# Causal linear attention: scores issued over four row groups, values kept stationary in four column groups, one PSUM ring of eight

## The chip, the cores and the metric

The kernel runs on one core of a Trainium2 chip. The metric is the device time of one execution in microseconds (us), lower is better. The core has a tensor engine (PE; its weight loads are listed apart as PEld), a vector engine (DVE), a scalar engine (ACT), a general engine (POOL), an engine that only issues transfers here (SP), and DMA engines that move data between device memory and the on-chip memory. Matrix products land in PSUM, from where DVE and ACT read them.

## The reference

The input x has 4 sequences of 1024 tokens with 256 channels. It is normalised, and two parts are added to it: an attention part and a mixture of experts. All arithmetic is in fp32.

```
xn = layernorm(x)
q, k, v = xn @ w_q.T, xn @ w_k.T, xn @ w_v.T        # 16 heads of 16 channels
sq, sk  = elu(q) + 1, elu(k) + 1
# causal linear attention, in chunks of 128 tokens, per head
scores = (sq_chunk @ sk_chunk.T) * lower_triangle
num = scores @ v_chunk + sq_chunk @ S
den = scores.sum(-1) + sq_chunk @ z
local = num / max(den, 1e-6)
S, z = S + sk_chunk.T @ v_chunk, z + sk_chunk.sum(0)
# memory output: sq against a coarse and four fine memories per head, mixed by gates
attn = (gate * memory + (1 - gate) * local) @ w_o.T
# experts: top 2 of 8 (176 hidden channels each), and a shared one with 352
out = x + attn + experts(xn) + shared(xn)
```

## The kernel before

The 4096 tokens are 32 tiles of 128, taken as 8 blocks of 4 tiles; two blocks are one sequence. The 16 heads are split into two halves c of 8 heads, each half on 128 channels (partitions). Head h of a half stands on partitions 16h to 16h+15, so two heads share each of four groups g of 32 partitions.

First all blocks are normalised and routed. Then the tokens are sorted by expert: 64 indirect DMAs on POOL (`scatter`, line 407) write rows to a sorted copy in device memory. There are 71 expert steps (`expert`, lines 779 to 809), each on 128 sorted rows with its own weights, loaded from SP two steps ahead (`fetch`). Each step is a transpose pair (pxg), a product (phe), an activation on ACT and DVE, another transpose pair (pTe) and a product (pye), with ACT copying between them, and its rows go out to device memory. At the end 64 indirect gathers on POOL (`combine`, line 815) bring two expert rows for each token back; DVE adds them and SP stores the result.

Attention of a block (`attention_units`) has four units for each of its tiles i:

- `scores(i)`: for each g, four products, two halves c and two heads r. They contract 16 partitions for the even head; for the odd head they contract 32, with a copy of the keys (skO) that is zero on the even head's rows. One PSUM tile sc holds the four results of a g, 128 keys by 128 queries each. DVE multiplies it with the causal mask into sT (line 535).
- `local(i)`: for each half, the state term, with the queries as the stationary operand and the state streamed (line 550), and then for each head a product with the masked scores as stationary operand (128 by 128) and the head's values and a column of ones, 17 columns, streamed (line 555). All land in one PSUM tile pn with tokens on partitions. DVE clips and inverts the denominators, and scales (lines 564 to 567).
- `update(i)`: keys are transposed, multiplied with the values, masked to each head's own rows on DVE (line 594) and added to the old state on POOL (line 598), except for the first tile of a sequence, which needs no addition.
- `memory(i)`: the products px and py with the memories, scaled on DVE (line 625, tile fm) and added on POOL (lines 630 and 631). fm has one buffer.

After four tiles come `expand_gate` and `mix`, which make the attention result. `shared_units` adds the shared expert and the output projection.

Blocks are overlapped by `together` (line 827): while block b has its shared units and block b+1 its attention, the expert steps of sixths of the 71 are dealt in between (blocks 0 to 5); in blocks 6 and 7 the combines are dealt in. The framework's scheduler then orders the instructions of each engine at compile time and gives each tile a buffer; SP alone keeps the order of the program. Each engine executes its queue in order.

PSUM has two pools of four tiles: ps_a for routing and attention, and ps_f for the experts and the shared part (lines 88 and 89).

Of the kernel before, what the change touches and what calls it, by code (L numbers as in the profile page):

```python
# [8 lines left out]
FP = mybir.dt.float32  # L9
# [5 lines left out]
P = 128  # L15
NT = 4
TB = P * NT
# [5 lines left out]
def linear_attention_moe_kernel(  # L23
# [28 lines left out]
    nc = tc.nc  # L52
    T, H = x.shape
    S = T // B
    NH = memory_gate.shape[1]
    HD = H // NH
    NC = H // P
    HC = NH // NC
    NG = HC // 2
    NM = memories.shape[1]  # L60
    D1 = HD + 1
    FR = E * F
    FT = w_gate.shape[1]
    FS = FT - FR
# [20 lines left out]
    exw = ctx.enter_context(tc.tile_pool(name="exw", bufs=3))  # L85
    exp = ctx.enter_context(tc.tile_pool(name="exp", bufs=2))
    dram = ctx.enter_context(tc.tile_pool(name="dram", bufs=1, space=bass.MemoryType.DRAM))
    ps_a = ctx.enter_context(tc.tile_pool(name="ps_a", bufs=4, space=bass.MemoryType.PSUM))
    ps_f = ctx.enter_context(tc.tile_pool(name="ps_f", bufs=4, space=bass.MemoryType.PSUM))

    st = {}

# [43 lines left out]
    if full < NF:  # L136
# [26 lines left out]
    nc.vector.tensor_reduce(  # L163
        odd, own.rearrange("p (g r) -> p g r", r=2)[:, :, 1], AX.X, ALU.add
    )

    own_s = const.tile([P, NC, HC * D1], FP, tag="own_s", name="own_s")
    for c in range(NC):
# [340 lines left out]
    def attention_units(blk):  # L509
# [6 lines left out]
                st[name, blk] = one.tile([P, NT, H], FP, tag=name, name=f"{name}_{blk}")  # L516

        def scores(i):
            sqT, skT, skO = st["sqT", blk], st["skT", blk], st["skO", blk]
            tok = slice(i * P, (i + 1) * P)  # L520
            for g in range(NG):
                even = slice(32 * g, 32 * g + HD)
                both = slice(32 * g, 32 * g + 2 * HD)
                sc = ps_a.tile([P, NC, 2, P], FP, tag="a", name=f"sc_{blk}_{i}_{g}")
                for c in range(NC):
                    nc.tensor.matmul(  # L526
                        sc[:, c, 0, :], skT[even, c, tok], sqT[even, c, tok],
                        start=True, stop=True,
                    )
                    nc.tensor.matmul(  # L530
                        sc[:, c, 1, :], skO[both, c, tok], sqT[both, c, tok],
                        start=True, stop=True,
                    )
                sT = tmp.tile([P, NC * 2, P], FP, tag="sT", name=f"sT_{blk}_{i}_{g}", bufs=4)
                nc.vector.tensor_mul(  # L535
                    sT,
                    sc.rearrange("p c r t -> p (c r) t"),
                    causal[:, None, :].to_broadcast([P, NC * 2, P]),
                )
                st["sT", g] = sT  # L540

        def local(i):
            sqT, va = st["sqT", blk], st["va", blk]
            tok = slice(i * P, (i + 1) * P)
            started = half > 0 or i > 0
            pn = ps_a.tile([P, 512], FP, tag="a", name=f"pn_{blk}_{i}")
            for c in range(NC):
                at = c * HC * D1
                if started:
                    nc.tensor.matmul(  # L550
                        pn[:, at : at + HC * D1], sqT[:, c, tok], st["state"][:, c, :],
                        start=True, stop=False,
                    )
                for h in range(HC):
                    nc.tensor.matmul(  # L555
                        pn[:, at + h * D1 : at + (h + 1) * D1],
                        st["sT", h // 2][:, c * 2 + h % 2, :],
                        va[:, i, c * HC + h, :],
                        start=not started,
                        stop=(not started) or h == HC - 1,  # L560
                    )
            pn3 = pn[:, : NH * D1].rearrange("p (h k) -> p h k", k=D1)
            rden = small.tile([P, NH], FP, tag="rden", name=f"rden_{blk}_{i}")
            nc.vector.tensor_scalar(rden, pn3[:, :, HD], EPS, None, ALU.max)  # L564
            nc.vector.reciprocal(rden, rden)
            nc.vector.tensor_mul(rden, rden, ungate)
            nc.vector.tensor_mul(
                st["local", blk][:, i, :].rearrange("p (h k) -> p h k", k=HD),
                pn3[:, :, :HD],
                rden[:, :, None].to_broadcast([P, NH, HD]),  # L570
            )

        def update(i):

            if half == BPB - 1 and i == NT - 1:
                return
            skT, va = st["skT", blk], st["va", blk]
            tok = slice(i * P, (i + 1) * P)
            pk = ps_a.tile([P, NC, P], FP, tag="a", name=f"pk_{blk}_{i}")
            for c in range(NC):  # L580
                nc.tensor.transpose(pk[:, c, :], skT[:, c, tok], ident)
            sk = tmp.tile([P, NC, P], FP, tag="sk", name=f"sk_{blk}_{i}")
            nc.scalar.copy(sk, pk)
            pu = ps_a.tile([P, 512], FP, tag="a", name=f"pu_{blk}_{i}")
            for c in range(NC):
                nc.tensor.matmul(  # L586
                    pu[:, c * HC * D1 : (c + 1) * HC * D1],
                    sk[:, c, :],
                    va[:, i, c * HC : (c + 1) * HC, :].rearrange("p h k -> p (h k)"),
                    start=True, stop=True,  # L590
                )
            old = st.get("state") if half > 0 or i > 0 else None
            new = tmp.tile([P, NC, HC * D1], FP, tag="state", name=f"state_{blk}_{i}")
            nc.vector.tensor_mul(  # L594
                new, pu[:, : NC * HC * D1].rearrange("p (c k) -> p c k", c=NC), own_s
            )
            if old is not None:
                nc.gpsimd.tensor_add(new, new, old)  # L598
            st["state"] = new

        def memory(i):
            sqT, w5 = st["sqT", blk], st["w5", b]
# [98 lines left out]
    def shared_units(blk):  # L701
        hid = {}

        def hidden(f):
            xnT = st["xnT", blk]
            n = min(P, FS - f * P)
            pg = ps_f.tile([P, TB], FP, tag="f", name=f"pg_{blk}_{f}")
            pu = ps_f.tile([P, TB], FP, tag="f", name=f"pu_{blk}_{f}")
            for ps, w in ((pg, wg), (pu, wu)):
                for k in range(NC):  # L710
                    nc.tensor.matmul(  # L711
                        ps[:n, :], w[:, k, f * P : f * P + n], xnT[:, k, :],
                        start=(k == 0), stop=(k == NC - 1),
                    )

            th = tmp.tile([P, TB], FP, tag="wide", name=f"th_{blk}_{f}", bufs=3)
            nc.scalar.activation(th[:n], pg[:n], AF.Tanh, scale=0.5)
            nc.vector.scalar_tensor_tensor(  # L718
                th[:n], th[:n], 1.0, pg[:n], ALU.add, ALU.mult
            )  # L720
            h = hidp.tile([P, TB], FP, tag="h", name=f"h_{blk}_{f}")
            nc.vector.scalar_tensor_tensor(  # L722
                h[:n], th[:n], 0.5, pu[:n], ALU.mult, ALU.mult
            )
            hid[f] = h

        def output(i):
            tok = slice(i * P, (i + 1) * P)
            rows = slice(blk * TB + i * P, blk * TB + (i + 1) * P)
            oT = st["oT", blk]  # L730
            if i == 0:
                st["acc", blk] = big.tile([P, NT, H], FP, tag="tok", name=f"acc_{blk}")
            res = tmp.tile([P, H], FP, tag="res", name=f"res_{blk}_{i}")
            nc.scalar.dma_start(res, x[rows, :])
            po = ps_f.tile([P, 512], FP, tag="f", name=f"po_{blk}_{i}")
            for c in range(NC):
                nc.tensor.matmul(  # L737
                    po[:, :H], oT[:, c, tok], wo[:, c, :], start=(c == 0), stop=False
                )
            for f in range(NF):  # L740
                n = min(P, FS - f * P)
                nc.tensor.matmul(  # L742
                    po[:, :H], hid[f][:n, tok], wd[:n, f, :],
                    start=False, stop=(f == NF - 1),
                )
            nc.vector.tensor_add(st["acc", blk][:, i, :], po[:, :H], res)
# [32 lines left out]
    def expert(j):  # L779
        rows = slice(j * P, (j + 1) * P)  # L780
        fetch(j + 2)
        wgu, wdn, xg = st.pop(("fetched", j))
        pt = ps_f.tile([P, NC, P], FP, tag="f", name=f"pxg_{j}")
        for c in range(NC):
            nc.tensor.transpose(pt[:, c, :], xg[:, c * P : (c + 1) * P], ident)
        xgT = exp.tile([P, NC, P], FP, tag="xgT", name=f"xgT_{j}")
        nc.scalar.copy(xgT, pt)  # L787
        ph = ps_f.tile([P, 2, F], FP, tag="f", name=f"phe_{j}")
        for k in range(NC):
            nc.tensor.matmul(  # L790
                ph.rearrange("p g f -> p (g f)"), xgT[:, k, :],
# [4 lines left out]
        nc.scalar.activation(th, ph[:, 0, :], AF.Tanh, scale=0.5)  # L796
        nc.vector.scalar_tensor_tensor(th, th, 1.0, ph[:, 0, :], ALU.add, ALU.mult)  # L797
        nc.vector.scalar_tensor_tensor(th, th, 0.5, ph[:, 1, :], ALU.mult, ALU.mult)
        pT = ps_f.tile([P, 2, P], FP, tag="f", name=f"pTe_{j}")
        for f in range(2):  # L800
            nc.tensor.transpose(pT[:FH, f, :], th[:, f * FH : (f + 1) * FH], ident)
        hT = exp.tile([FH, 2, P], FP, tag="hTe", name=f"hTe_{j}")
        nc.scalar.copy(hT, pT[:FH])  # L803
        py = ps_f.tile([P, H], FP, tag="f", name=f"pye_{j}")
        for f in range(2):
            nc.tensor.matmul(py, hT[:, f, :], wdn[:, f, :], start=(f == 0), stop=(f == 1))  # L806
        y = exp.tile([P, H], FP, tag="row", name=f"y_{j}", bufs=5)
# [119 lines left out]
```

## Time and profile before

| what | value |
|---|---|
| median of 14 runs | 1132.08 us (1130.59 to 1143.23) |
| the profiled execution | 1128.23 us, span 1126.5 us |
| PE busy | 1010.0 us, 90% |
| DVE, POOL and ACT busy | 468.2, 237.4 and 210.1 us |
| mean granted clock of PE | 0.831 |
| value products, line 555 | 1024 records, mean 327 ns, busy 186.4 us |
| score products, lines 526 and 530 | 1024 records, busy 87.7 and 83.4 us |
| state term, line 550 | 112 records, busy 35.2 us |
| causal mask, line 535 | 128 instructions, mean 685 ns |

The span runs from the first to the last instruction of the program. "Granted clock" is the share of full speed at which PE was allowed to run. Busy time of a group is the union of its instructions' intervals; since matmuls are pipelined, groups that follow each other closely overlap, and their busy times add up to more than the time that passed. What a step takes on PE is better read from when its records start. The chain of waits is followed back from the last instruction: each piece is what the next one waited for.

### The profile page before, as it was taken

To read this page: it belongs to the slowest core of one execution; us is meant where nothing else is said; L and a number is where in the kernel's file an instruction comes from. 1 tells how busy PE (TensorE), PEld (TensorE's weight loads), DVE (VectorE), ACT (ScalarE), POOL (GpSimd) and SP (SyncE) were. 2 spreads that over 40 slices of the span, in tenths; PEclk is the share of its full clock that TensorE was granted. 3 is DMA by queue.
4 is the path that set the end of the run, shared out by engine and by line. 5 is a ranking of instruction groups with operands and counts; after the bars stand their busy time and mean duration, and the time that the engine had idled before them with its cause. 6 is when DMAs were issued, how large, how long until landed. Compare 5 with 4: busy or idle time off the path is not lost.

```text
span 1126.5 us, 13616 instructions
## 1 busy us (share of the span) xinstructions
PE 1010.0 (90%) x4644; PEld 754.3 (67%) x4644; DVE 468.2 (42%) x1382; ACT 210.1 (19%) x522; POOL 237.4 (21%) x261
## 2 busy tenths in 40 slices
PE   4879419899799999999899999899989999999986
PEld 3757317688466787677656788578746788667653
DVE  5775114342333434434343334432333424435765
ACT  1222000101234112111134210221124311110010
POOL 1117772010100011001100011100110001106865
PEclk9998657576899768997899876997699866898888
DMA  9713230112224212232223321232132421102345
GB/s 294 254 54 107 103 115 24 36 45 58 86 68 126 83 37 64 57 93 73 84 67 112 100 73 42 62 101 74 58 86 82 122 74 42 49 24 82 119 135 146
DMA packets 105234, 98.86 MB, mean 88 GB/s; under 512 B 10781, under 2 KB 101069, under 8 KB 105165
## 3 DMA queue, kind: packets, MB, share of 16 engines
q1 hardware_dynamic: 81181, 65.41, 20.0%
q0 software_dynamic: 6144, 16.79, 4.8%
q10 hardware_dynamic: 17840, 15.79, 4.4%
q8 instruction: 37, 0.61, 0.2%
q14 instruction: 32, 0.26, 0.1%
HBM read 66.75 MB, written 31.20 MB: 87 GB/s over the span
## 4 chain that ended last, share of the span: by engine, by line
PE 76%; POOL 9%; DVE 7%; issue 3%; DMA 3%; ACT 2%; ACTq 0%; POOLq 0%; DVEq 0%
PE pn L555 14%; PE phe L790 10%; POOL xs L407 5%; PE pye L806 5%; PE sc L526 5%; PE py L624 4%; PE po L742 3%; PE sc L530 3%; PE pu L711 3%; PE pl L293 2%; PE pg L711 2%; PE pn L550 2%; PE po L737 2%; PE px L606 2%; PE pu L586 2%
## 5 line engine op out<-in xcount | busy, mean ns | idle before, releaser
L555 PEld LDWEIGHTS pn<-va,sT 128*128 128x128 f32 x1024 | 192.4, 283 | 4.1 <-issue 1.5
L555 PE MATMUL pn<-va,sT 128*128 128x17 f32 x1024 | 186.4, 327 | 0.0
L790 PE MATMUL phe<-wgu,xgT 128*128 128x352 f32 x284 | 125.7, 574 | 2.7 <-ACT xgT L787 2.4
L526 PE MATMUL sc<-sqT,skT 16*128 16x128 f32 x512 | 87.7, 309 | 40.3 <-DVE fm L625 39.6
L630 POOL TENSOR_TENSOR fm<-fm 128x512 f32<-128x512 f32 x32 | 40.6, 1269 | 347.3 <-DVE fm L625 188.2
L535 DVE TENSOR_TENSOR sT<-sc,causal 128x512 f32<-128x512 f32 x128 | 84.7, 685 | 62.5 <-PE sc L530 62.0
L526 PEld LDWEIGHTS sc<-sqT,skT 16*128 16x128 f32 x512 | 64.2, 192 | 61.4 <-DVE fm L625 41.9
L790 PEld LDWEIGHTS phe<-wgu,xgT 128*128 128x128 f32 x284 | 61.1, 234 | 38.3 <-issue 14.0
L530 PE MATMUL sc<-sqT,skO 32*128 32x128 f32 x512 | 83.4, 282 | 0.0
L806 PE MATMUL pye<-wdn,hTe 88*128 88x256 f32 x284 | 81.0, 410 | 1.0 <-ACT hTe L803 0.9
L564 DVE TENSOR_SCALAR rden<-pn 128x16 f32<-128x16 f32 x32 | 5.6, 174 | 176.7 <-PE pn L555 176.7
L598 POOL TENSOR_TENSOR state<-state,state 128x272 f32<-128x272 f32 x24 | 18.5, 770 | 280.7 <-DVE state L594 212.5
L624 PE MATMUL py<-mem_y,sqT 128*128 128x512 f32 x128 | 72.3, 669 | 0.0
L407 POOL DMA_INDIRECT xs<-x,is x64 | 61.8, 965 | 41.6 <-DVE is L392 22.4
L530 PEld LDWEIGHTS sc<-sqT,skO 32*128 32x128 f32 x512 | 66.4, 195 | 6.1 <-issue 6.1
L806 PEld LDWEIGHTS pye<-wdn,hTe 88*128 88x128 f32 x284 | 54.1, 201 | 24.0 <-ACT hTe L803 15.4
L815 POOL DMA_INDIRECT yt<-ys,is x64 | 62.2, 971 | 22.4 <-DVE acc L821 8.6
L797 DVE SCALAR_TENSOR_TENSOR the<-the,phe 128x176 f32<-128x176 f32 x71 | 23.7, 334 | 100.1 <-ACT the L796 100.0
L625 DVE TENSOR_TENSOR fm<-py,rw 128x512 f32<-128x512 f32 x64 | 43.6, 682 | 42.6 <-POOL fine L631 40.1
L796 ACT ACTIVATE the<-phe 128x176 f32<-128x176 f32 x71 | 22.6, 318 | 184.7 <-PE phe L790 181.2
L711 PE MATMUL pg<-xnT,wg 128*128 128x512 f32 (+1 forms) x96 | 51.5, 661 | 5.4 <-DVE th L718 5.4
L742 PE MATMUL po<-wd,h 128*128 128x256 f32 (+1 forms) x192 | 48.3, 386 | 2.0 <-DVE h L722 2.0
(174 smaller groups left out, 1446.3 us busy)
## 6 DMA issues: line engine op xcount, KB each, us to landing
wgu<-in_w_gate_dram SPq DMA_DIRECT2D x71, 176.0 KB
wgu<-in_w_up_dram SPq DMA_DIRECT2D x71, 176.0 KB
wdn<-in_w_down_dram SPq DMA_DIRECT2D x71, 176.0 KB
xs<-zero SPq DMA_DIRECT2D x71, 128.0 KB
xg<-xs SPq DMA_DIRECT2D x71, 128.0 KB
ys<-y ACTq DMA_DIRECT2D x71, 128.0 KB
x<-in_x_dram SPq DMA_DIRECT2D x8, 512.0 KB
res<-in_x_dram ACTq DMA_DIRECT2D x32, 128.0 KB
```

The source lines that it names most:

```text
L407: put = nc.gpsimd.indirect_dma_start(out=xs, out_offset=bass.IndirectOffsetOnAxis(ap=islot[r][:, i : i + 1], axis=0), in_=st["x", i // NT] ...
L526: nc.tensor.matmul(sc[:, c, 0, :], skT[even, c, tok], sqT[even, c, tok], start=True, stop=True,)
L530: nc.tensor.matmul(sc[:, c, 1, :], skO[both, c, tok], sqT[both, c, tok], start=True, stop=True,)
L535: nc.vector.tensor_mul(sT, sc.rearrange("p c r t -> p (c r) t"), causal[:, None, :].to_broadcast([P, NC * 2, P]),)
L555: nc.tensor.matmul(pn[:, at + h * D1 : at + (h + 1) * D1], st["sT", h // 2][:, c * 2 + h % 2, :], va[:, i, c * HC + h, :], start=not start ...
L624: nc.tensor.matmul(py, sqT[:, c, tok], mem_y[:, c, :], start=True, stop=True)
L625: nc.vector.tensor_mul(fm[:, c].rearrange("p m (h k) -> p (m h) k", k=HD), py.rearrange("p (n k) -> p n k", k=HD), rw[:, c, HC:, None].to_ ...
L711: nc.tensor.matmul(ps[:n, :], w[:, k, f * P : f * P + n], xnT[:, k, :], start=(k == 0), stop=(k == NC - 1),)
L742: nc.tensor.matmul(po[:, :H], hid[f][:n, tok], wd[:n, f, :], start=False, stop=(f == NF - 1),)
L790: nc.tensor.matmul(ph.rearrange("p g f -> p (g f)"), xgT[:, k, :], wgu[:, k].rearrange("p g f -> p (g f)"), start=(k == 0), stop=(k == NC ...
L806: nc.tensor.matmul(py, hT[:, f, :], wdn[:, f, :], start=(f == 0), stop=(f == 1))
L815: nc.gpsimd.indirect_dma_start(out=yt, out_offset=None, in_=ys, in_offset=bass.IndirectOffsetOnAxis(ap=islot[r][:, i : i + 1], axis=0),)
```

## The change

The change edits the scores, the local step and the state, and joins the PSUM pools.

- `scores(i)` takes four PSUM tiles at once, one for each g, and goes through halves c and heads r outside and g inside, so that four successive products lie in four different groups of 32 partitions. The masks follow after all sixteen products.
- `local(i)` swaps the operands. The heads are taken in four quarters q of four heads. For each quarter the state is stationary (128 by 128: four heads of 32 columns, 17 of them used) and the queries are streamed. For each head the values (128 by 17) are stationary and the masked scores, 128 columns, are streamed; the four heads of a quarter write to partitions 0, 32, 64 and 96 of pn. pn now has channels on partitions, so ACT copies it out, and four transposes bring it back into a new PSUM tile pb, from where DVE goes on as before.
- The state lives in two fixed buffers with 32 columns a head, cleared by POOL at the start. The first tile of a sequence uses the zeros; at the end of a sequence the next buffer is cleared again by POOL. `update` writes every other buffer and always adds the old one.
- One PSUM pool of eight tiles serves everything.

```diff
+    CW = 32
...
-    ps_a = ctx.enter_context(tc.tile_pool(name="ps_a", bufs=4, space=bass.MemoryType.PSUM))
-    ps_f = ctx.enter_context(tc.tile_pool(name="ps_f", bufs=4, space=bass.MemoryType.PSUM))
+    ps_a = ctx.enter_context(tc.tile_pool(name="ps_a", bufs=8, space=bass.MemoryType.PSUM))
+    ps_f = ps_a
...
+    states = [
+        const.tile([P, NC, HC, CW], FP, tag=f"state{k}", name=f"state{k}") for k in range(2)
+    ]
+    for state in states:
+        nc.gpsimd.memset(state, 0.0)
...
+            sc = [
+                ps_a.tile([P, NC, 2, P], FP, tag="a", name=f"sc_{blk}_{i}_{g}")
+                for g in range(NG)
+            ]
+            for c in range(NC):
+                for r, keys in enumerate((skT, skO)):
+                    for g in range(NG):
+                        rows = slice(32 * g, 32 * g + (1 + r) * HD)
+                        nc.tensor.matmul(
+                            sc[g][:, c, r, :], keys[rows, c, tok], sqT[rows, c, tok],
+                            start=True, stop=True,
+                        )
...
+            state = states[(half * NT + i) % 2]
+            nq = NH // 4
+            pn = ps_a.tile([P, nq, P], FP, tag="a", name=f"pn_{blk}_{i}")
+            for q in range(nq):
+                c, h0 = divmod(4 * q, HC)
+                nc.tensor.matmul(
+                    pn[:, q, :],
+                    state[:, c, h0 : h0 + 4, :].rearrange("p h k -> p (h k)"),
+                    sqT[:, c, tok],
+                    start=(q == 0), stop=False, skip_group_check=True,
+                )
+            for q in range(nq):
+                for r in range(4):
+                    c, h = divmod(4 * q + r, HC)
...
+                        pn[CW * r : CW * r + D1, q, :],
+                        va[:, i, c * HC + h, :],
+                        st["sT", h // 2][:, c * 2 + h % 2, :],
+                        start=False, stop=(q == nq - 1), skip_group_check=True,
...
+            nT = tmp.tile([P, nq, P], FP, tag="wide", name=f"nT_{blk}_{i}", bufs=3)
+            nc.scalar.copy(nT, pn)
+            pb = ps_a.tile([P, nq, P], FP, tag="a", name=f"pb_{blk}_{i}")
+            for q in range(nq):
+                nc.tensor.transpose(pb[:, q, :], nT[:, q, :], ident)
+            pn3 = pb.rearrange("p q (r k) -> p (q r) k", k=CW)
...
+            if n == BPB * NT - 1:
+                nc.gpsimd.memset(new, 0.0)
                 return
...
+            nc.gpsimd.tensor_add(
+                new[:, :, :, :D1], new[:, :, :, :D1], old[:, :, :, :D1]
+            )
```

More of the change, by code (lines that the diff above doesn't have):

```diff
@@ L520, in scores @@
             tok = slice(i * P, (i + 1) * P)
-            for g in range(NG):
[L522 to L533, printed above, removed]
+            sc = [
[10 more added lines that the diff above has]
+                        )
+            for g in range(NG):
                 sT = tmp.tile([P, NC * 2, P], FP, tag="sT", name=f"sT_{blk}_{i}_{g}", bufs=4)
@@ L536, in scores @@
                     sT,
-                    sc.rearrange("p c r t -> p (c r) t"),
+                    sc[g].rearrange("p c r t -> p (c r) t"),
                     causal[:, None, :].to_broadcast([P, NC * 2, P]),
@@ L544, in local @@
             tok = slice(i * P, (i + 1) * P)
[L545 to L549, printed above, removed]
+            state = states[(half * NT + i) % 2]
[12 more added lines that the diff above has]
+                    c, h = divmod(4 * q + r, HC)
                     nc.tensor.matmul(
-                        pn[:, at : at + HC * D1], sqT[:, c, tok], st["state"][:, c, :],
-                        start=True, stop=False,
-                    )
[L554 to L562, printed above, removed]
+                        pn[CW * r : CW * r + D1, q, :],
+                        va[:, i, c * HC + h, :],
+                        st["sT", h // 2][:, c * 2 + h % 2, :],
+                        start=False, stop=(q == nq - 1), skip_group_check=True,
+                    )
+            nT = tmp.tile([P, nq, P], FP, tag="wide", name=f"nT_{blk}_{i}", bufs=3)
[4 more added lines that the diff above has]
+            pn3 = pb.rearrange("p q (r k) -> p (q r) k", k=CW)
             rden = small.tile([P, NH], FP, tag="rden", name=f"rden_{blk}_{i}")
@@ L573, in update @@
         def update(i):
-            if half == BPB - 1 and i == NT - 1:
+            n = half * NT + i
+            old, new = states[n % 2], states[(n + 1) % 2]
+            if n == BPB * NT - 1:
+                nc.gpsimd.memset(new, 0.0)
                 return
@@ L591, in update @@
                 )
-            old = st.get("state") if half > 0 or i > 0 else None
-            new = tmp.tile([P, NC, HC * D1], FP, tag="state", name=f"state_{blk}_{i}")
             nc.vector.tensor_mul(
-                new, pu[:, : NC * HC * D1].rearrange("p (c k) -> p c k", c=NC), own_s
-            )
-            if old is not None:
-                nc.gpsimd.tensor_add(new, new, old)
-            st["state"] = new
+                new[:, :, :, :D1],
+                pu[:, : NC * HC * D1].rearrange("p (c h k) -> p c h k", c=NC, k=D1),
+                own_s.rearrange("p c (h k) -> p c h k", k=D1),
+            )
+            nc.gpsimd.tensor_add(
+                new[:, :, :, :D1], new[:, :, :, :D1], old[:, :, :, :D1]
+            )
         def memory(i):
@@ L706, in hidden @@
             n = min(P, FS - f * P)
-            pg = ps_f.tile([P, TB], FP, tag="f", name=f"pg_{blk}_{f}")
-            pu = ps_f.tile([P, TB], FP, tag="f", name=f"pu_{blk}_{f}")
+            pg = ps_f.tile([P, TB], FP, tag="a", name=f"pg_{blk}_{f}")
+            pu = ps_f.tile([P, TB], FP, tag="a", name=f"pu_{blk}_{f}")
             for ps, w in ((pg, wg), (pu, wu)):
@@ L734, in output @@
             nc.scalar.dma_start(res, x[rows, :])
-            po = ps_f.tile([P, 512], FP, tag="f", name=f"po_{blk}_{i}")
+            po = ps_f.tile([P, 512], FP, tag="a", name=f"po_{blk}_{i}")
             for c in range(NC):
@@ L782, in expert @@
         wgu, wdn, xg = st.pop(("fetched", j))
-        pt = ps_f.tile([P, NC, P], FP, tag="f", name=f"pxg_{j}")
+        pt = ps_f.tile([P, NC, P], FP, tag="a", name=f"pxg_{j}")
         for c in range(NC):
@@ L787, in expert @@
         nc.scalar.copy(xgT, pt)
-        ph = ps_f.tile([P, 2, F], FP, tag="f", name=f"phe_{j}")
+        ph = ps_f.tile([P, 2, F], FP, tag="a", name=f"phe_{j}")
         for k in range(NC):
@@ L798, in expert @@
         nc.vector.scalar_tensor_tensor(th, th, 0.5, ph[:, 1, :], ALU.mult, ALU.mult)
-        pT = ps_f.tile([P, 2, P], FP, tag="f", name=f"pTe_{j}")
+        pT = ps_f.tile([P, 2, P], FP, tag="a", name=f"pTe_{j}")
         for f in range(2):
@@ L803, in expert @@
         nc.scalar.copy(hT, pT[:FH])
-        py = ps_f.tile([P, H], FP, tag="f", name=f"pye_{j}")
+        py = ps_f.tile([P, H], FP, tag="a", name=f"pye_{j}")
         for f in range(2):
```

## The prediction

> **What bounds the kernel now.** I read the page's busy times first, then the chain of waits, then windows, and last the timeline of single steps.
>
> ```profile
> PE 1010.0 (90%) x4644; PEld 754.3 (67%) x4644; DVE 468.2 (42%) x1382; ACT 210.1 (19%) x522; POOL 237.4 (21%) x261
> PEclk9998657576899768997899876997699866898888
> PE 76%; POOL 9%; DVE 7%; issue 3%; DMA 3%; ACT 2%; ACTq 0%; POOLq 0%; DVEq 0%
> PE pn L555 14%; PE phe L790 10%; POOL xs L407 5%; PE pye L806 5%; PE sc L526 5%; PE py L624 4%; PE po L742 3%; PE sc L530 3%; PE pu L711 3%; PE pl L293 2%; PE pg L711 2%; PE pn L550 2%; PE po L737 2%; PE px L606 2%; PE pu L586 2%
> ```
>
> The tensor engine carries three quarters of the chain. The value products (pn, line 555) are its largest item, and the scores (sc, lines 526 and 530) and the state term (line 550) are edited too. The granted clock is often near half.
>
> ```profile
> 165.00:1020.00 855.00, 820.10 (x3794) 613.91 (x3794) 320.03 (x838) 175.60 (x446) 87.30 (x88) 0.83 0.25 70
> 543.80:547.20 3.40, 3.40 (x18) 3.40 (x18) 0.00 (x0) 0.00 (x0) 0.00 (x0) 0.50 0.00 0
> 343.00:363.00 20.00, 20.00 (x79) 12.78 (x77) 6.42 (x17) 10.68 (x27) 0.00 (x0) 1.00 0.45 125
> ```
>
> These are windows: length, then busy time of PE, weight loads, DVE, ACT and POOL, granted clock, DMA. From 165 to 1020 us PE idles only 35 us of 855. Inside a value step (second line) the clock is 0.50; in a stretch of projections and experts it is 1.00. Mean 0.83 means 2 x 0.17 x 855 = 291 us at half clock.
>
> ```profile
> 517.82 3.44 PE L555 MATMUL pn<-va,sT 128*128 128x17 f32 x16
> 479.05 1.86 PE L555 MATMUL pn<-va,sT 128*128 128x17 f32 x16
> ```
>
> Each fp32 matmul leaves two records (1024 for 512 in the page's groups), a transpose one. Sixteen records take 3.23 us on the chain at half clock (202 ns each); the full-clock example takes 1.86 us, about 110 each. Only 17 columns stream: the 128-column weight load sets this pace.
>
> ```profile
> 535.90 0.37 PE L530 MATMUL sc<-sqT,skO 32*128 32x128 f32 x1
> 535.90 0.37 PE L526 MATMUL sc<-sqT,skT 16*128 16x128 f32 x1
> 536.11 0.27 PE L530 MATMUL sc<-sqT,skO 32*128 32x128 f32 x1
> 536.12 0.27 PE L526 MATMUL sc<-sqT,skT 16*128 16x128 f32 x1
> 536.23 0.38 PE L530 MATMUL sc<-sqT,skO 32*128 32x128 f32 x2
> 536.45 0.49 PE L526 MATMUL sc<-sqT,skT 16*128 16x128 f32 x4
> 536.67 0.49 PE L530 MATMUL sc<-sqT,skO 32*128 32x128 f32 x4
> 537.01 0.38 PE L526 MATMUL sc<-sqT,skT 16*128 16x128 f32 x3
> ```
>
> This decides the scores. The last product of one 32-row group and the first of the next start together at 535.90 and again at 536.11: two row groups run at once. Inside a group records follow at 110 ns. The pattern repeats after 0.56 us (536.45 to 537.01) for eight records, 70 ns each, so neighbours overlap in part already.
>
> ```profile
> PE sc L526 <- DVE fm L625: 39.6, 1, 39.6
> ```
>
> From the waits: near 125 us PE stops for 40 us. The chain there is POOL's 64 scatters, 1.27 us apart, 80 to 161 us. Its end is as fixed: 64 gathers 1.25 us apart run on POOL from 1022 to 1120 us.
>
> **The change part by part.** I sum over 165 to 1020 us, which holds 27 token tiles (864 value records of 32 a tile). The chain narrowed to it gives pn 16.9%, sc 5.4 and 4.1%, state term 2.9%: 29.3% of 855 = 250 us, 9.3 us a tile.
>
> Scores. Sixteen matmuls become four sets over four row groups. If four overlap as two do at 535.90, a set takes two records, 0.22 us: 0.9 us. Entering and leaving the 32-row shape costs about 0.3 us (the first score record lasts 372 ns against 270; a full product follows the last one after 0.2 instead of 0.11). I take 1.2 us; if never more than two overlap it is 16 x 0.11 + 0.3 = 2.1.
>
> State term. Four matmuls with 128 streamed columns replace two with 136: 8 records x 0.11 = 0.9 us. It runs on the first tile of a sequence too, against zeros.
>
> Values. 32 records now stream 128 score columns, 0.11 us each, into four column groups, with 17-column weights. The trace has no column groups. Bounds: four at once, 8 x 0.11 + 0.2 = 1.1 us; one after another, 32 x 0.11 + 0.2 = 3.7. Nearest are the row groups, which do overlap, so I take 1.3.
>
> Back-transposes. Four records, 0.44 us, and 0.2 for the change of shape: 0.65. Sum: 1.2 + 0.9 + 1.3 + 0.65 = 4.05, with another 0.05 for gaps 4.1 us. Bounds: 3.85 and 7.35. Saved: 5.2 x 27 = 140 us (147 to 53).
>
> Clock. If 63% of 864 records run at 202 ns and the rest at 107, they make the 144 us it has on the chain; so pn holds about 110 us of the 291 half-clock microseconds and the state term some 20. The other 160 is work such as phe, px and pu, which follows a value step at half clock (phe x4 takes 2.71 us at 526 us). At full clock it would take 80 less. The new step streams 128 columns for 17, like the scores, which stay at 1.00; I count 60 (0 to 80).
>
> New waits. The four masks (line 535, 685 ns each) follow each score group today. Now all four score tiles finish together, so 4 x 0.69 = 2.7 us of DVE stands before the values, some 1.9 us more than today. Then an ACT copy of 128x512 (588 ns in line 648's rows) precedes the transposes, and the reads by line 564 come after those: 0.8 us. Uncovered that is 2.7 x 27 = 73 us. The cover is update, memory and 1.1 to 1.9 experts a tile, all independent. In blocks with few experts it is thin. I charge 30 us (0 to 100, the last with the stalls of a shared PSUM ring).
>
> PSUM. The scores hold four PSUM tiles at once out of one ring of eight, where attention had four of its own and experts four; the experts' tiles can queue behind score tiles that wait for DVE. It can gain or lose; it is in the charge for waits.
>
> First tiles. The update of tile 0 now ends in a POOL add that local(1) needs. POOL's queue has the scatters before it, so tile 1's values, about 4 us, and its update and memory, 3 us, move behind the 40 us stall: +7 us.
>
> Others. ACT gains 32 x 0.59 = 19 us at 19% load; POOL four adds of 0.77 us and small memsets, which in its queue stand ahead of later additions; DVE reads the same counts with other strides. All hide under PE, and uncovered would be 22 us (19 and 4 x 0.77). SP's queue of expert loads does not change. Experts come faster: 71 in some 690 us is 9.8 us each, while 343 to 363 us shows 6.2 with DMA at 0.45. The tail after the last expert, 104 us, is POOL's gathers: 0 (5 either way).
>
> Sum against the profiled execution's 1128.23 us (span 1126.5 and 1.7 around it): 1128.2 - 140 - 60 + 30 + 7 = 965. The median shown is 3.9 above that execution: 969, I say 970.
>
> **Two rules against it.** The Trainium skill, TensorE: Matmul & The Clock Gate, Part 3, says a weight load overlaps a running matmul only when its row group differs. The column groups here all use every row group, so by that rule alone values would take about 3.7 us, and the total 970 + 27 x 2.4 = 1035. The same part states 2.38 times for three column tiles, by which it would be near 1.6 us. No row here shows either. TensorEngine Tiling (Array Packing), Key Properties, says changing the tiling mode drains the engine; the rows agree, 0.2 us after a score instead of 0.11.
>
> **The rivals.** *Columns run one after another*, at full clock: 3.7 for 1.3 us, 1035 us. For it: no column group in the trace; against it: row groups overlap.
>
> *The waits are not covered*: 100 us for 30 and a third of the clock gain lost: 970 + 70 + 20 = 1060. For it: DVE's 320 us would then fill 46% of some 690, with masks in bursts; against it: PE idles only 4% now.
>
> *Slower than before*: columns in turn and still half clock. Local costs 32 x 0.21 + 8 x 0.21 + 4 x 0.21 and 0.4 for shapes, 9.6 us, and scores 2.1: 11.7 a tile, +65 us, no clock gain, waits 30 and first tile 7: 1132 + 102 = 1234. It decides once local passes 9.3 - 2.1 - 1.4 (waits by tile) = 5.8 us. Against it: scores stream the same 128 columns and run at 1.00.
>
> *The groups don't work at all*: neither scores nor values overlap. Scores 3.8, local 5.3, together 9.1 a tile: -5 us; a third of the clock gain, -20, and waits and first tile, +37, give 1144; with half of it, 1134, no difference.
>
> **How the numbers follow.** Forecast 55%, 970, own range 905 to 1010 (low: 1132 - 147 - 80 + 0 + 0 = 905; high: waits up to 70). Columns in turn 18%; waits 14%; slower 8%; groups not working 5%, of which 2 is no difference. The range needs 8 in 10: 895 to 1070 takes in the first three cases, a little below the lower bound for POOL's tail. Within 0.3% is what a measurement of this kernel can't tell from no change. Faster 0.87, same 0.02, slower 0.11.
>
> **What would show it.** In the changed profile: four score records starting within 30 ns; a score set in 0.22 us; value records near 30 ns apart (110 would be columns in turn); PEclk of the steady stretch at 0.93 or more; PE idle there near 65 us rather than 35; line 407's scatters still ending near 161 us; the gathers still 1.25 us apart. The prediction is wrong if value records stand 110 ns or more apart, if the clock in a value step stays at 0.50, or if PE waits over 3 us a tile for masks or PSUM.

## The result and the profile after

The changed kernel takes 1309.63 us (median of 10 runs, 1293.55 to 1326.27), the kernel before 1134.27 us (47 runs). The ratio is 1.149, 95% interval 1.1452 to 1.1528: 15% slower, where 970 us was forecast. Some executions of a kernel run longer at a lower granted clock, and the ratios here leave these out.

The page of the changed kernel, busy times, granted clock by slice, and the chain of waits by engine and by line:

```profile
PE 917.7 (70%) x4916; PEld 579.2 (44%) x4916; DVE 478.6 (37%) x1382; ACT 232.1 (18%) x554; POOL 244.0 (19%) x271
PEclk9996596887998978786799897998779988797679
PE 58%; DVE 15%; ACT 10%; POOL 8%; issue 5%; DMA 4%; ACTq 0%; POOLq 0%; SPq 0%; DVEq 0%
PE phe L812 8%; PE pye L828 7%; POOL xs L414 5%; PE pg L733 4%; DVE sT L544 3%; PE pu L733 3%; PE po L764 3%; PE pn L570 3%; PE py L646 3%; PE sc L538 2%; PE pTe L823 2%; PE ph L681 2%; PE pl L300 2%; DMA yt<-ys,is 2%; PE po L759 2%
```

PE is busy 92 us less than before, though the kernel takes 175 us more. The value products are now line 570 and fell from 14% of the chain to 3%; the scores (line 538) fell from 8% to 2%. DVE rose from 7% of the chain to 15% and ACT from 2% to 10%, with little more work of their own (busy 479 and 232 us instead of 468 and 210). So PE now waits for short steps of other engines. The steady stretch as one window (length, busy time of PE, weight loads, DVE, ACT and POOL, granted clock, DMA share, GB/s):

```profile
165.00:1170.00 1005.00, 745.81 (x3969) 457.96 (x3967) 326.10 (x835) 193.19 (x470) 91.69 (x94) 0.86 0.21 59
```

PE idles 259 us of 1005, against 35 of 855 before. Where, the list of PE's waits shows (who waited, for whom, us, times, longest):

```profile
PE pTe L823 <- DVE the L820: 83.1, 68, 1.4
PE pn L561 <- POOL state L619: 59.9, 3, 54.6
PE poT L665 <- POOL local L712: 50.0, 8, 7.9
PE phe L812 <- ACT xgT L809: 35.6, 71, 0.8
PE pye L828 <- ACT hTe L825: 32.5, 71, 0.5
PE ph L681 <- ACT cT L670: 28.6, 8, 6.9
PE pb L580 <- ACT nT L577: 22.1, 32, 0.7
PE pn L570 <- DVE sT L544: 16.7, 41, 4.7
```

The three waits inside an expert step (phe, pTe, pye) make 151 us, on nearly all of the 71 steps. Before they made 14 us:

```profile
PE pTe L801 <- DVE the L798: 10.5, 9, 3.4
PE phe L790 <- ACT xgT L787: 2.4, 5, 0.5
PE pye L806 <- ACT hTe L803: 0.9, 2, 0.5
```

They are the largest part of the new idle time, but not all of it: the waits for POOL's mixing (poT, 50.0 instead of 8.5 us) and for the ACT copy before ph (28.6 instead of 8.1) grew too, and those for masks and copy in the new local step (pn L570 and pb) make 39 us. The long wait of 54.6 us at L561 lies ahead of this stretch. The timeline of one expert step in the changed kernel, PE alone:

```profile
273.74 0.38 PE L807 MATMUL pxg<-ident,xg 128*128 128x128 f32 x2
274.58 1.45 PE L812 MATMUL phe<-wgu,xgT 128*128 128x352 f32 x4 [0.46 <-ACT xgT L809]
277.28 0.39 PE L823 MATMUL pTe<-ident,the 128*88 128x128 f32 x2 [1.24 <-DVE the L820]
278.13 1.13 PE L828 MATMUL pye<-wdn,hTe 88*128 88x256 f32 x4 [0.46 <-ACT hTe L825]
```

Nothing stands between the four parts: PE waits for ACT's copy, for ACT and DVE together, and for a copy again, 2.2 us a step. Before, other matmuls filled those places, as between phe, pTe and pye of this step (phe runs at half clock here, 2.71 us for 1.45):

```profile
526.09 2.71 PE L790 MATMUL phe<-wgu,xgT 128*128 128x352 f32 x4
528.60 1.11 PE L586 MATMUL pu<-va,sk 128*128 128x136 f32 x4
529.50 1.20 PE L606 MATMUL px<-mem_x,sqT 128*128 128x168 f32 x4
530.54 1.02 PE L624 MATMUL py<-mem_y,sqT 128*128 128x512 f32 x2
531.40 0.38 PE L801 MATMUL pTe<-ident,the 128*88 128x128 f32 x2
531.62 1.02 PE L624 MATMUL py<-mem_y,sqT 128*128 128x512 f32 x2
532.48 1.03 PE L806 MATMUL pye<-wdn,hTe 88*128 88x256 f32 x4
```

The edited steps themselves did what they were meant to do. Scores and values of one tile on PE:

```profile
267.97 0.50 PE L538 MATMUL sc<-sqT,skT 16*128 16x128 f32 x8
268.30 0.40 PE L538 MATMUL sc<-sqT,skO 32*128 32x128 f32 x8
268.52 0.40 PE L538 MATMUL sc<-sqT,skT 16*128 16x128 f32 x8
268.74 0.40 PE L538 MATMUL sc<-sqT,skO 32*128 32x128 f32 x8
269.07 1.16 PE L561 MATMUL pn<-sqT,state 128*128 128x128 f32 x8
270.16 0.77 PE L570 MATMUL pn<-sT,va 128*17 128x128 f32 x8
271.13 0.40 PE L570 MATMUL pn<-sT,va 128*17 128x128 f32 x4 [0.20 <-DVE sT L544]
271.73 0.84 PE L570 MATMUL pn<-sT,va 128*17 128x128 f32 x20 [0.20 <-DVE sT L544]
273.25 0.33 PE L580 MATMUL pb<-ident,nT 128*128 128x128 f32 x1 [0.69 <-ACT nT L577]
```

After the first set, each set of four score matmuls (eight records) starts 0.22 us after the one before it, where two records in one row group took that long: four row groups run at once. The last 20 value records take 0.84 us including the end of the last, where one after another at 0.11 us they would take 2.2: four column groups run at once too. What lies between is waiting for masks.

The order that the scheduler compiled says why. It is read from the compiled programs, not from a trace; the traces agree (no record of another matmul stands inside any of the 71 expert steps of the changed kernel). "Late" counts PSUM tiles whose first matmul comes after that of a tile which the program made later; "inside" is the mean number of other matmuls on PE between the first and the last of an expert's eight.

```
kernel                          late, all tiles   late, within one pool   inside an expert
before (pools of 4 and 4)            319                   0                    12.4
changed (one ring of 8)                0                   0                     0.0
before with the ring alone             0                   0                     2.0
changed, pools of 4 and 4            396                   0                    16.4
changed, pools of 5 and 3            372                   0                    14.7
changed, ring, experts dealt           0                   0                    17.5
```

Within one pool, PSUM tiles are first written strictly in the order in which the program makes them, in every kernel of the table. Two pools let the scheduler slide the experts' tiles against attention's. One pool takes that freedom away: PE's order becomes that of the program, where an expert step is one block.

### The profile page after: what moved, and what is told of

It reads as the page before. It is cut to its first block, busy times and chain, and to the rows that moved or that the text cites. A ratio compares the mean times of both kernels' runs of the same rounds, so it can differ in the third digit from the quotient of the medians.

```text
span 1302.3 us, 14287 instructions
## 1 busy us (share of the span) xinstructions
PE 917.7 (70%) x4916; PEld 579.2 (44%) x4916; DVE 478.6 (37%) x1382; ACT 232.1 (18%) x554; POOL 244.0 (19%) x271
## 4 chain that ended last, share of the span: by engine, by line
PE 58%; DVE 15%; ACT 10%; POOL 8%; issue 5%; DMA 4%; ACTq 0%; POOLq 0%; SPq 0%; DVEq 0%
PE phe L812 8%; PE pye L828 7%; POOL xs L414 5%; PE pg L733 4%; DVE sT L544 3%; PE pu L733 3%; PE po L764 3%; PE pn L570 3%; PE py L646 3%; PE sc L538 2%; PE pTe L823 2%; PE ph L681 2%; PE pl L300 2%; DMA yt<-ys,is 2%; PE po L759 2%
## 5 line engine op out<-in xcount | busy, mean ns | idle before, releaser
L812 PE MATMUL phe<-wgu,xgT 128*128 128x352 f32 x284 | 109.4, 510 | 35.6 <-ACT xgT L809 35.6
L828 PE MATMUL pye<-wdn,hTe 88*128 88x256 f32 x284 | 92.0, 452 | 32.5 <-ACT hTe L825 32.5
L561 PE MATMUL pn<-sqT,state 128*128 128x128 f32 x256 | 48.5, 348 | 59.9 <-POOL state L619 59.9
L823 PE MATMUL pTe<-ident,the 128*88 128x128 f32 x142 | 29.2, 288 | 86.9 <-DVE the L820 83.1
L570 PE MATMUL pn<-sT,va 128*17 128x128 f32 x1024 | 65.9, 330 | 16.9 <-DVE sT L544 16.7
L561 PEld LDWEIGHTS pn<-sqT,state 128*128 128x128 f32 x256 | 41.3, 245 | 65.0 <-POOL state L619 60.5
L823 PEld LDWEIGHTS pTe<-ident,the 128*88 128x88 f32 x142 | 11.8, 124 | 126.7 <-issue 92.8
L577 ACT COPY nT<-pn 128x512 f32<-128x512 f32 x32 | 18.8, 586 | 273.9 <-PE pn L570 273.9
L570 PEld LDWEIGHTS pn<-sT,va 128*17 128x17 f32 x1024 | 34.0, 112 | 43.0 <-DVE sT L544 35.1
L809 ACT COPY xgT<-pxg 128x256 f32<-128x256 f32 x71 | 26.4, 372 | 143.7 <-PE pxg L807 127.4
L665 PE MATMUL poT<-ident,local 128*128 128x128 f32 x64 | 15.7, 427 | 50.0 <-POOL local L712 50.0
```

What stands on the lines that cost most here:

```text
L561: nc.tensor.matmul(pn[:, q, :], state[:, c, h0 : h0 + 4, :].rearrange("p h k -> p (h k)"), sqT[:, c, tok], start=(q == 0), stop=False, ski ...
L570: nc.tensor.matmul(pn[CW * r : CW * r + D1, q, :], va[:, i, c * HC + h, :], st["sT", h // 2][:, c * 2 + h % 2, :], start=False, stop=(q == ...
L812: nc.tensor.matmul(ph.rearrange("p g f -> p (g f)"), xgT[:, k, :], wgu[:, k].rearrange("p g f -> p (g f)"), start=(k == 0), stop=(k == NC ...
```

## The experiments

Three theories stood at the start. *Order*: the single ring fixes PE's order and so exposes the experts' latencies. *Own waits*: the new steps lose the time themselves, by masks, copy and back-transposes. *Sharing*: tiles for scores and experts run short in a common ring.

### The ring alone, and the change without the ring

The kernel before, with this edit:

```diff
-    ps_a = ctx.enter_context(tc.tile_pool(name="ps_a", bufs=4, space=bass.MemoryType.PSUM))
-    ps_f = ctx.enter_context(tc.tile_pool(name="ps_f", bufs=4, space=bass.MemoryType.PSUM))
+    ps_a = ctx.enter_context(tc.tile_pool(name="ps_a", bufs=8, space=bass.MemoryType.PSUM))
+    ps_f = ps_a
```

> The kernel before, with the one PSUM ring of eight as the only edit. Theory: the single ring is what makes the scheduler put each unit's matmuls back to back on PE (in the changed kernel an expert's eight matmuls have no other between them, in the kernel before 12.4 on average, here 2.0), so PE waits out each expert's ACT and DVE steps. Then this kernel alone is slower than before by 100 to 250 us, 1230 to 1380 us, with PE idle in the steady stretch of 130 us or more against 35. Rival (the new steps' own waits for masks, copy and transposes cost the time, the ring is harmless): within 15 us of 1134.

Measured: ratio 1.3278 (1.3227 to 1.3328), 1508.64 us. The ring alone costs 374 us, more than was expected. Its steady stretch:

```profile
165.00:1364.00 1199.00, 975.95 (x3699) 682.70 (x3700) 327.88 (x827) 178.81 (x444) 86.64 (x87) 0.71 0.18 50
```

Idle is 223 us instead of 35, and PE is busy for 976 us instead of 820 with about the same matmuls (3699 records in this stretch against 3794), while the clock falls from 0.83 to 0.71; by the clock alone, 820 us would become 959 (820 x 0.83 / 0.71). The ring costs twice: by waits and by the clock. The three waits inside the experts make 145 us here too (pTe 82.4, pye 32.5, phe 29.6).

The changed kernel with the two pools kept:

```diff
-    ps_a = ctx.enter_context(tc.tile_pool(name="ps_a", bufs=8, space=bass.MemoryType.PSUM))
-    ps_f = ps_a
+    ps_a = ctx.enter_context(tc.tile_pool(name="ps_a", bufs=4, space=bass.MemoryType.PSUM))
+    ps_f = ctx.enter_context(tc.tile_pool(name="ps_f", bufs=4, space=bass.MemoryType.PSUM))
...
-            pg = ps_f.tile([P, TB], FP, tag="a", name=f"pg_{blk}_{f}")
+            pg = ps_f.tile([P, TB], FP, tag="f", name=f"pg_{blk}_{f}")
```

and so for every tile of ps_f; the other two kernels have five and three, and six and two.

> The changed kernel with the two pools of four kept as before (experts and shared part on their own four tiles). Theory that the ring orders PE: the expert's steps interleave with attention again, and the scores and values keep their new price, so 950 to 1030 us. Rival (the new steps' own waits): it stays at 1250 us or more.

> The changed kernel with two pools, five tiles for attention and three for experts and shared part. Scores hold four tiles at once, and with four in all nothing of the same attention can run beside them; a fifth lets one update, memory or value tile pass. Theory of the ring: 940 to 1030 us, up to 30 us better than four and four if the scores' four tiles starve attention, worse if experts and shared part need the fourth. Rival (own waits): 1250 us or more.

> The changed kernel with two pools, six tiles for attention and two for experts and shared part. Theory of the ring: still far under before, 940 to 1060 us, since an expert uses one tile after the other and two are enough for it; the shared part's pairs would be serial on two tiles, some 10 to 20 us. Rival (own waits): 1250 us or more.

Measured: four and four 0.8813 (0.8789 to 0.8836), 1000.41 us; five and three 0.8665 (0.8638 to 0.8692), 982.45 us; six and two 0.8828 (0.8791 to 0.8865), 999.77 us. *Own waits* falls: the same new steps are 12 to 13% faster than before once the pools are apart. Against five and three the ring costs 1.149 - 0.8665 = 0.283 of 1134 us, 320 us, on top of the new steps; against four and four, the pools that the kernel before had, 0.268 or 304 us. Five and three was run a second time, as the measure for later kernels:

> The changed kernel with pools of five and three once more, as the measure for the next two. Expected ratio to before 0.86 to 0.87.

It gave 0.8682 (0.8637 to 0.8728). Its chain and steady stretch:

```profile
PE 60%; DVE 12%; POOL 11%; issue 8%; DMA 5%; ACT 4%; ACTq 0%; POOLq 0%; SPq 0%; DVEq 0%
```

```profile
165.00:865.00 700.00, 648.67 (x4041) 412.29 (x4040) 321.96 (x839) 189.40 (x470) 91.78 (x94) 0.98 0.30 85
```

Idle is 51 us and the clock 0.98. Against the ring's 1005 us, 305 us are gone: 208 of idling and 97 of PE's busy time, on about the same matmuls (4041 records against 3969). The clock alone would take 91 of these 97 (746 x 0.86 / 0.98 = 655). The place of the expert's parts now, from its timeline of PE:

```profile
430.84 0.38 PE L807 MATMUL pxg<-ident,xg 128*128 128x128 f32 x2
431.16 0.50 PE L538 MATMUL sc<-sqT,skT 16*128 16x128 f32 x6
431.74 1.45 PE L812 MATMUL phe<-wgu,xgT 128*128 128x352 f32 x4
433.12 0.37 PE L538 MATMUL sc<-sqT,skT 16*128 16x128 f32 x1
...
434.35 0.42 PE L823 MATMUL pTe<-ident,the 128*88 128x128 f32 x2 [0.51 <-DVE the L820]
434.69 0.50 PE L538 MATMUL sc<-sqT,skT 16*128 16x128 f32 x6
435.22 1.13 PE L828 MATMUL pye<-wdn,hTe 88*128 88x256 f32 x4
```

The scores are cut up and stand between the expert's parts. A tile's 32 score records take longer this way than in one piece, but PE waits 0.51 us in this step instead of 2.2.

### The ring kept, the order changed in the program

If the order is the loss, the ring can stay where the program itself deals finer. `expert` returns four parts instead of running as one, and `together` deals these:

```diff
         side = [
-            lambda j=j: expert(j)
+            part
             for j in range(blk * NST // busy, min(NST, (blk + 1) * NST // busy))
+            for part in expert(j)
         ]
...
+        return [turn, up, back, down]
```

> The changed kernel with its one ring of eight, but each expert step is cut in the program into its four parts (transposes in; product and activation; transposes back; second product), and the parts are dealt one by one between the attention and shared units. Theory that a pool gives out PSUM tiles in the order of the program and that this order was the loss: 950 to 1020 us, as with two pools, though the ring is kept. Rival (sharing eight tiles between experts and scores is itself the loss, by waits for banks): 1150 us or more.

The second kernel also changes the order of attention's units, with the second half of `local` (copy, back-transposes, scaling) as a unit of its own, `back`:

```diff
-            units += [lambda i=i: scores(i), lambda i=i: local(i)]
-            units += [lambda i=i: update(i), lambda i=i: memory(i)]
+            units += [lambda i=i: scores(i), lambda i=i: update(i)]
+            units += [lambda i=i: local(i), lambda i=i: memory(i), lambda i=i: back(i)]
```

> As the dealt experts on one ring, and in each tile update stands between scores and values, and memory between values and their copy and back-transposes, so that other matmuls stand where PE waits for masks and for the copy. Theory of the order: 10 to 30 us better than the dealt experts alone, 930 to 1000 us. Rival (waits for banks): 1150 or more.

Measured, against a kernel before that took 1170.03 us on that chip: experts dealt 0.9491 (0.9419 to 0.9564); with the moved units 0.903 (0.8941 to 0.912). The ratio falls from 1.149 by 0.20 and 0.25 with the ring of eight untouched. So about 0.246 of the ring's 0.283 comes back by order alone, as far as ratios of two chips can be compared. Both miss what was expected: scaled to the usual chip the first is 1076 us (0.9491 x 1134) where 950 to 1020 was expected, the second 1024 where 930 to 1000 was. Steady stretch of the second:

```profile
165.00:930.00 765.00, 633.76 (x4097) 424.75 (x4098) 336.27 (x858) 188.94 (x473) 94.48 (x97) 0.93 0.27 78
```

It still idles 131 us, against 51 with two pools. Whether the remaining 0.037 is a dealing by hand that is coarser than the scheduler's, or the sharing of eight tiles, these runs do not tell apart.

The same move of units, with pools of five and three, asks whether attention's own waits cost anything there:

> Pools of five and three, and in the program update stands between scores and values, and memory between values and their copy and back-transposes. Since a pool gives its tiles out in program order, attention's own order decides what stands in PE's queue while DVE masks the scores and ACT copies pn. If those waits still cost something (PE idles 53 us in the steady stretch with five and three), this takes 10 to 40 us off: ratio 0.83 to 0.86. If experts already cover them, no difference to five and three (within 5 us).

Measured: 0.8675 (0.8637 to 0.8712), 984.30 us, no difference to five and three in the same comparison (0.8682). With the scheduler free to fill in, the waits for masks and copy are covered.

### The parts of the change alone

> The kernel before with the new values, state and back-transposes alone; pools of four and four, scores as before. The value records fall from 167 ns to about 55 (3.5 us a tile less), the state term and transposes cost about 1.0 us more, and the clock should come back to 0.9 or more, worth some 70 us: 27 x 2.5 + 70, minus a few for the copy: 980 to 1020 us. If the gain of the two changes together (134 us) needs both, 1040 or more with a clock still under 0.88.

This kernel is the one with pools of four and four, with the old `scores`. Measured: 0.8869 (0.8802 to 0.8936), 1038.07 us where the kernel before took 1170.03; scaled to 1134 us that is 1006, in the expected range. The new values alone bring nearly as much as both parts with these pools (0.8813):

```profile
165.00:915.00 750.00, 699.39 (x4163) 479.70 (x4164) 331.76 (x868) 189.59 (x476) 94.60 (x97) 0.93 0.28 80
```

The clock rises from 0.83 to 0.93.

> The kernel before with the new scores alone (16 products with the group innermost, four PSUM tiles at once); pools of four and four, values and state as before. In the changed kernel a tile's 32 score records start within 0.91 us, against about 3.3 us in the steady stretch before: 27 tiles x 2 us = 55 us less, part of it lost to masks that all wait for the last set. The value step keeps the clock at half. Expected 1070 to 1115 us. If the row groups are worth nothing here, since the old order overlapped in part and the four tiles fill the pool, 1125 to 1160.

> The new scores alone on pools of four and four, again, since the first profile was a disturbed one. The row groups' price: 27 tiles x 2 us less, with the clock at half in the value step as before: ratio 0.92 to 0.98. If the old overlap was worth as much, 0.99 to 1.02.

The edit is the new `scores` in the kernel before. The first set gave no ratio; its median was 1082.3 us beside 1170.03. The second gave 0.9128 (0.9064 to 0.9192), from two of its four runs (1031.77 and 1039.35 us). This is a larger gain than expected: 9% from the row groups alone. The two parts do not add up: 0.8869 and 0.9128 would make 0.81, and together they give 0.8813 with the same pools. The granted clock of the whole executions points to a reason: 0.82 to 0.83 before, 0.90 in these two runs, 0.90 with the new values alone, 0.92 with both. Each part alone wins most of the clock that both together win, and the expectation that the clock stays at half in the value step did not hold. That this accounts for all that is missing is not shown.

> The kernel before with its two pools cut five and three instead of four and four, nothing else. If the 18 us by which five and three beat four and four in the changed kernel come from the scores' four tiles held at once, there is no such gain here: ratio 0.99 to 1.01. If three tiles for the experts and five for attention are simply the better cut, 0.98 or less.

Measured: 0.9962 (0.9925 to 1.0). So the cut of five and three is worth at most 0.8% in the kernel before, and 1.5% in the changed one (0.8665 against 0.8813). That fits four score tiles held at once, which fill a pool of four; the runs show no more than that.

## Why the prediction was wrong

**The step that failed** is the paragraph on PSUM: "It can gain or lose; it is in the charge for waits". That charge was 30 us, 0 to 100 with the stalls of the ring. The ring alone cost 304 to 320 us. The forecast asked whether eight tiles are enough, and never asked what else the two pools did. They were the only thing that allowed the scheduler to move experts against attention. The trace of before already held the signs: expert and attention matmuls stood inside each other's steps (pTe between the py above), so PE did not follow the program. That the experts' waits were small for that reason, 14 us, the ring alone then showed: there they make 145.

**"The cover is update, memory and 1.1 to 1.9 experts a tile, all independent."** They are independent in data, but in one pool they are not free to move. This sentence named the right cover and missed the condition on which it stands. With two pools the idle time was 51 us, where 65 was forecast; with the ring it was 259.

**Scores, values, back-transposes.** Right. A score set was forecast at 0.22 us and takes 0.22; in the tile above the scores take 1.1 us (1.2 forecast), the state term 1.1 (0.9) and the four back-transposes 0.66 (0.65). Value records were forecast near 30 ns apart where four overlap; in the kernel with five and three, groups of four start 0.11 to 0.12 us apart, with 7 ns between most neighbours, and 32 records that only an expert's transposes interrupt take 1.3 us (1.3). The rule of the Trainium skill (TensorE: Matmul & The Clock Gate, Part 3) that a weight load overlaps a running matmul only when its row group differs would have made this 110 ns a record; the column groups share all row groups and overlap all the same. The same part's measured gain for three column tiles points the right way, and here the measurement decides.

**Clock.** The size was right, but it hung on a condition that was not named. The term was 60 us, out of 160 half-clock microseconds beside the new step. With five and three the stretch runs at 0.98, which leaves some 28 of the 291 half-clock microseconds (2 x 0.02 x 700); if all of these lie beside the step, 132 of the 160 went, worth 66 us. In the ring the clock is 0.86, which is 281 us at half clock (2 x 0.14 x 1005), as many as before, though the value step is short. There the clock falls to half 45 times in the steady stretch, and in the 3.4 us ahead of a fall PE was busy for half of the time in the median and never above 0.68; in 35 of the 45 at least half of its work there was an expert's. Two windows of the changed kernel, ahead of a fall and behind it:

```profile
387.43:390.84 3.41, 1.71 (x7) 0.83 (x6) 0.71 (x3) 0.69 (x2) 0.00 (x0) 1.00 0.38 105
390.84:394.26 3.42, 3.42 (x9) 2.72 (x9) 0.00 (x0) 0.74 (x2) 0.00 (x0) 0.50 0.34 92
```

With five and three the clock falls three times. The prediction's argument that scores stream 128 columns and "stay at 1.00" also missed what follows the old scores: in the kernel with new values and old scores, 12 of the 15 falls come after 3.4 us of which the scores fill at least 0.65, with PE busy 0.84 or more.

**First tiles.** The wait came as foreseen: PE waits 54.6 us for a state addition on POOL behind the scatters, where it waited 39.6 before. Its price of 7 us was not measured alone.

**Tail.** Forecast unchanged within 5 us. From the last expert product to the end it took 107 us before, 132 with the ring and 113 with five and three. In the ring the gathers begin 4 us after that product (3 before) but take 122 us instead of 98: they wait 29.0 us for DVE's additions, where they waited 8.6 before. Why those additions are late was not followed.

**The rivals.** The one that ended slower named columns in turn at half clock, which did not happen; uncovered waits were priced at 1060 us, by masks and copy alone. The right mechanism was uncovered waits, but most of all those of the experts (151 us), which the change does not touch; masks and copy make 39 us, 1.2 us a tile, far under the 3 us a tile that was named as a sign of being wrong. The forecast for the new steps by themselves, 970 us, is within 1.3% of the 982 us that they reach with pools of five and three, and 3.1% under the 1000 us with four and four. That closeness is partly luck: in the steady stretch PE's busy time fell by 171 us where 140 and 60 were forecast, and its idle time rose by 16 where 30 was charged.

## What to carry to other kernels

A buffer pool is also an order: where a scheduler hands out a pool's tiles in the order of the program, two pools are two streams that can slide past each other, and joining them for more buffers each makes one stream. Before joining pools, look on the bounding engine for work of one standing inside units of the other, and price the waits that would be bare without it; here that was 2.2 us for each of 71 experts, and the clock on top. Where a change bundles a good step with such a join, take the join out: the changed kernel with pools of five and three runs in 982 us, 13% faster than before; no kernel of this study is clearly faster.

## What the hardware showed that was not expected

Records of small fp32 products in four row groups or four column groups mostly start 7 ns apart, and a group of four takes the 0.11 us of a single record, with weights of 17 columns as with 128. And an order with idle gaps cost clock as well as time: with unchanged matmuls the ring alone took the granted clock of the steady stretch from 0.83 to 0.71 and PE's busy time from 820 to 976 us. Of the 59 falls of the clock there, 44 come after 3.4 us in which PE was busy for at most 0.70 of the time, in 37 of them at least half of it with an expert's matmuls; 11 others come after 3.4 us of which the old scores fill half or more.
